# A four-layer cross-attention stack: 128x128 block products by Winograd's seven-product scheme in queries and outputs, and other buffers around layer 1's feed-forward part

## The chip, the cores and the metric

The kernel runs on one core of one Trainium2 chip. The core has five engines with a queue of instructions each: TensorE (PE), which multiplies matrices and loads its stationary operand by separate instructions (PEld), VectorE (DVE), ScalarE (ACT), GpSimd (POOL) and SyncE (SP), whose queue issues most of the DMAs. The metric is the device time of one execution in microseconds (us). All data are float32; one matmul of the program is two PE instructions.

## The reference

`x` is (4, 256, 256): four batch entries of 256 tokens of width 256. `ctx` is (4, 512, 128). Four layers each add a cross-attention and a feed-forward part (FFN), both on a layernormed `x`:

```
x = x + xattn_L(layernorm(x), ctx)
x = x + ffn_L(layernorm(x))            # L = 0, 1, 2, 3
```

Layer 0's attention has 16 heads of 16 and normed queries and keys, and its FFN picks 4 of 64 low-rank products per token. The attention of layers 1 to 3, which the change concerns, is

```
q = x @ Wq -> 16 heads of 128;   k, v = ctx @ Wk, ctx @ Wv -> 8 heads, each used by two
out = softmax(q @ k.T / sqrt(128)) @ v @ Wo
```

The FFN of layer 1 is a mixture of eight experts with two per token (hidden width 176) and a shared one; that of layer 2 has two experts, one of which is chosen per token; that of layer 3 runs for the 64 tokens of each batch entry that score highest in a router, and leaves the others.

## The kernel before

**Folded weights.** For layers 1 to 3 no keys and values are made. `folding` (L957) multiplies the weights of each head h once: `m_sb` holds Wq_h Wk_h^T / sqrt(128) (256x128) and `n_sb` holds Wv_h Wo_h (128x256). A head's scores are then ctx (M_h^T x), its output (p ctx) N_h. The weights for it come in four groups of four DMAs (`load_raw`, L941) into a pool of raw buffers.

**`attention` (L1674).** The work is cut into units (b, hp): one batch entry and one pair of heads, 32 per layer, 96 in all. `queries` multiplies M of two heads (as stationary 128x128 blocks) with the 256 tokens (`xnT`, transposed, 128x256 moving) into a PSUM bank `pq`, and ScalarE copies that to `qT` (128x512). It runs one unit ahead. `heads` makes the scores `ps` in four blocks of 128 context rows, their exponentials `pT` (ScalarE), the product `po` with the context, and its copy `oT`; POOL begins the sum of the exponentials (`half`, 128x1024). `summed` ends that sum on DVE (add, 32x32 transposes `turned`, reduction into `sums`). Four head pairs make a quarter here: `quotients` sums over partitions with PE (`pz`), takes reciprocals (`rz`), spreads them to `wide` with DVE and multiplies four `oT` by them, on POOL. It runs in head pair 5 for the first quarter of an entry, and in head pair 1 of the next entry for its second. `output` multiplies `oT` (stationary) with N (256 columns) over all 16 heads into a bank `py`, in head pair 3 of the next entry, one token tile of 128 after the other, and DVE adds it to `x_sb`. The layernorm of the next entry is spread over head pairs 2 (`Norm`, statistics), 4 (`tokens`) and 6 (`layernorm_T`: four PE transposes and a copy).

**The order of the work.** In these stages the orders of PE, ACT, DVE and POOL are those of the program text (`tc.manual_schedule`): what is written first stands first in the engine's queue. SP's order is the framework's. PSUM has eight banks: tags "s" (4), "mm" (2), "o" and "t" (1 each). A tile waits until the reads of the tile that had its buffer before are done; the buffers of a pool that is opened later may lie in the memory of a closed one, and then wait for what used that. A hook `after(b, hp)` puts pieces of the next FFN into units: layernorm and routing of entry b-1 in head pairs 4 to 7 of entry b (`beside1`, L1940; `beside2`, L2280; `beside3`, L2550, which has also pieces in head pairs 0 to 2). Of layer 3's router, `weights` ends with `diag` (L2436, DVE), which `spread` multiplies by ones (`pw`, L2443, PE).

**Layer 1's FFN** (from L1955). `Shared` units are the shared expert. `ranks`, `lists`, `listed` and `indices` make the list of rows for each expert (PE matmul `plist`, DVE). Then 23 blocks of 128 rows: each `Block` gathers its rows `xg` by an indirect DMA from `xd` in DRAM (POOL queue, four ahead), and writes its result to `yd` (SP queue). `Back` (L2162) gathers for each of eight token tiles its two rows from `yd` into `yg` (two indirect DMAs), and adds them to `x_sb`. It runs beside the fold of layer 2's weights, which PE does. Weights of the FFN come early into a pool `fwp` that is open from before attention 1. `load_raw(2, i)` (L2201) stands behind `indices` in the program.

Of the kernel before, what the change touches and what calls it, by code (L numbers as in the profile page):

```python
# [835 lines left out]
def bounded_path(ctx: ExitStack, tc: tile.TileContext, t, out: bass.AP, over):  # L836
# [815 lines left out]
    fwp = ctx.enter_context(tc.tile_pool(name="fwp", bufs=1))  # L1652
# [21 lines left out]
    def attention(L, m_sb, n_sb, first_xnT=None, after=None, at_end=None):  # L1674
# [4 lines left out]

        with tc.tile_pool(name=f"att{L}", bufs=2) as ap:  # L1680
            xnTs, xns, norms, qTs, outs, sums = {}, {}, {}, {}, {}, {}
            units = [(b, hp) for b in range(B) for hp in range(H // 2)]

            def queries(b, hp):
                u = f"{L}_{b}_{hp}"
                pq = bank("mm", [P, 2, S], f"pq{u}")
                for j in range(2):
                    for d in range(ND):
                        nc.tensor.matmul(  # L1689
                            pq[:, j, :],  # L1690
                            lhsT=m_sb[:, d, 2 * hp + j, :],
                            rhs=xnTs[b][:, d, :],
                            start=(d == 0),
                            stop=(d == ND - 1),
                        )
                qTs[b, hp] = ap.tile([P, 2 * S], F32, tag="qT", name=f"qT{u}")
                nc.scalar.copy(qTs[b, hp], pq.rearrange("p j s -> p (j s)"))  # L1697

            def heads(b, hp):
                u = f"{L}_{b}_{hp}"  # L1700
                pT = ap.tile([P, NK, 2 * S], F32, tag="pT", name=f"pT{u}")
                for k in range(NK):
                    ps = bank("s", [P, 2 * S], f"ps{u}_{k}")
                    nc.tensor.matmul(  # L1704
                        ps, lhsT=cT[:, b, k * P : (k + 1) * P], rhs=qTs[b, hp], start=True, stop=True
                    )
                    nc.scalar.activation(pT[:, k, :], ps, AF.Exp, bias=mbias[:, b, k : k + 1])  # L1707
                po = bank("o", [P, 2 * S], f"po{u}")
# [4 lines left out]
                raw = ap.tile([P, 2 * S], F32, tag="oT", name=f"oT{u}", bufs=H // 2 + 5)  # L1713
                nc.scalar.copy(raw, po)  # L1714
                outs.setdefault(b, []).append(raw)
# [15 lines left out]
            def quotients(b, quarter, last=False):  # L1731
# [10 lines left out]
                rz = ap.tile([P, 4, NB], F32, tag="rz", name=f"rz{u}")  # L1742
                nc.vector.tensor_scalar(rz, pz, 1.0e-37, None, ALU.max)  # L1743
                nc.vector.reciprocal(rz, rz)
                for i in range(4):
                    wide = ap.tile([P, NB, 32], F32, tag="turned", name=f"wide{u}_{i}")
                    nc.vector.transpose(wide, rz[:, i, :, None].to_broadcast([P, NB, 32]))  # L1747
# [935 lines left out]
```

## Time and profile before

Three runs took 1537.48, 1537.2 and 1531.69 us: median 1537.2. The profiled execution took 1532.39 us; its span, from the first to the last instruction of the trace, is 1530.6, and the rest lies around it. The mean granted clock of PE in it is 0.988 of full speed.

| engine | busy us | share of the span | instructions |
|---|---|---|---|
| PE | 1481.0 | 97% | 6243 |
| PEld | 935.2 | 61% | 6243 |
| DVE | 644.9 | 42% | 1357 |
| ACT | 589.1 | 38% | 1047 |
| POOL | 474.8 | 31% | 354 |

| stage | span, us | PE busy, us |
|---|---|---|
| attention 1 | 251 to 587 | 332.0 |
| FFN 1, shared expert and lists | 587 to 631 | 41.2 |
| FFN 1, blocks | 631 to 696 | 64.7 |
| FFN 1, rows back; fold; start of attention 2 | 696 to 740 | 38.4 |
| attention 2 | 740 to 1050 | 307.7 |
| FFN 2 and fold | 1050 to 1146 | 94.4 |
| attention 3 | 1146 to 1460 | 309.0 |
| end of attention 3 and FFN 3 | 1460 to 1530 | 59.1 |

In the profile's lines an instruction is named by its line in the kernel, its engine, and its tiles (out<-in, buffer numbers left out). In a group line there follow partitions x elements, the count, busy time in us and the mean in ns of one, then the idle time of the engine just before them and what ended it. In the timeline each line begins with start and duration in us; for several matmuls in a row the duration runs to the modelled end of the last, so the distance to the next start is the better measure. A line of waits has the total, the count and the longest. In a line of windows there follow, after the stretch, its length and the busy time and count of PE, PEld, DVE, ACT and POOL, PE's granted clock, the DMA share and GB/s.

### The profile page before, as it was taken

The page shows a single profiled execution, that of the slowest core. Times are in us where ns is not written, and L with a number is a line of the kernel's source. Part 1 is how long each engine was busy: PE and PEld are TensorE (multiplying, and loading weights), DVE is VectorE, ACT ScalarE, POOL GpSimd, SP SyncE. Part 2 cuts the span into 40 slices and gives each one's busy share as a digit, 9 for nine tenths or more (in the row PEclk, how much of TensorE's full clock was granted, in tenths as well). Part 3 has the DMA queues.
Part 4 walks back from the last instruction along what each step waited for, and adds up shares of the span by engine and source line. Part 5 has one row for each costly group of instructions (what it writes and reads, how often), then busy time and mean ns, then how long its engine had stood idle before and what let it go on. Part 6 is the DMA issues. An engine that isn't in the chain of part 4 may idle for free.

```text
span 1530.6 us, 16401 instructions
## 1 busy us (share of the span) xinstructions
PE 1481.0 (97%) x6243; PEld 935.2 (61%) x6243; DVE 644.9 (42%) x1357; ACT 589.1 (38%) x1047; POOL 474.8 (31%) x354
## 2 busy tenths in 40 slices
PE   8999998999999999999999999999999999999997
PEld 7665676556565567656455656566885565565656
DVE  5666863233534435424233332425442334324363
ACT  4666332442434433234444342422234433423221
POOL 2222343243434331324244342423002343423330
PEclk9999999999999999999999999999999999999999
DMA  4000223100000003135000000000410000000000
GB/s 159 1 1 2 69 69 126 16 0 0 7 1 7 0 3 115 56 86 163 7 0 1 0 1 0 1 0 3 140 55 1 0 1 0 0 1 1 0 0 31
DMA packets 39955, 43.15 MB, mean 28 GB/s; under 512 B 3833, under 2 KB 36826, under 8 KB 39868
## 3 DMA queue, kind: packets, MB, share of 16 engines
q1 hardware_dynamic: 36892, 35.85, 7.4%
q0 software_dynamic: 1872, 5.11, 1.2%
q8 instruction: 52, 0.85, 0.2%
q10 hardware_dynamic: 1104, 1.05, 0.2%
q14 instruction: 35, 0.29, 0.1%
HBM read 36.89 MB, written 5.11 MB: 27 GB/s over the span
## 4 chain that ended last, share of the span: by engine, by line
PE 84%; DVE 9%; POOL 3%; issue 2%; ACT 1%; DMA 0%; POOLq 0%; DVEq 0%; ACTq 0%
PE ps L1704 20%; PE po L1710 20%; PE pq L1689 10%; PE py L1760 10%; PE ph L2308 2%; PE po L2345 2%; PE pgu L2130 2%; PE ps L1313 2%; PE po L1323 2%; PE pyf L1440 1%; POOL oT L1751 1%; PE pyr L2155 1%; PE paf L1390 1%; DVE wide L1747 1%; POOL yg L2169 1%
## 5 line engine op out<-in xcount | busy, mean ns | idle before, releaser
L1717 POOL TENSOR_TENSOR half<-pT 128x1024 f32<-128x1024 f32 x96 | 225.0, 2344 | 579.1 <-ACT pT L1707 406.9
L1704 PE MATMUL ps<-qT,cT 128*128 128x512 f32 x768 | 350.1, 599 | 3.8 <-ACT qT L1697 3.8
L1710 PE MATMUL po<-pT,c_sb 128*128 128x512 f32 x768 | 345.3, 592 | 0.0
L1707 ACT ACTIVATE pT<-ps,mbias 128x512 f32<-128x512 f32 x384 | 263.3, 687 | 77.9 <-PE ps L1704 68.0
L1710 PEld LDWEIGHTS po<-pT,c_sb 128*128 128x128 f32 x768 | 146.0, 190 | 183.6 <-issue 183.1
L1704 PEld LDWEIGHTS ps<-qT,cT 128*128 128x128 f32 x768 | 147.7, 193 | 149.7 <-issue 140.6
L1723 DVE TENSOR_TENSOR half<-half 128x512 f32<-128x512 f32 x96 | 75.0, 782 | 357.4 <-POOL half L1717 357.4
L1689 PE MATMUL pq<-xnT_a,m_sb 128*128 128x256 f32 x768 | 183.4, 383 | 0.7 <-ACT xnT_a L923 0.7
L1760 PE MATMUL py<-n_sb,oT 128*128 128x256 f32 x768 | 169.3, 380 | 1.3 <-POOL oT L1751 1.3
L1689 PEld LDWEIGHTS pq<-xnT_a,m_sb 128*128 128x128 f32 x768 | 143.6, 191 | 39.8 <-issue 14.1
L1760 PEld LDWEIGHTS py<-n_sb,oT 128*128 128x128 f32 x768 | 145.4, 190 | 26.1 <-issue 4.8
L1714 ACT COPY oT<-po 128x512 f32<-128x512 f32 x96 | 56.2, 585 | 263.4 <-PE po L1710 263.4
L1697 ACT COPY qT<-pq 128x512 f32<-128x512 f32 x96 | 56.1, 585 | 255.5 <-PE pq L1689 246.5
L1751 POOL TENSOR_TENSOR oT<-oT,wide 128x512 f32<-128x512 f32 x90 | 121.0, 1375 | 67.3 <-DVE wide L1747 67.3
L1317 ACT ACTIVATE pT<-ps 128x512 f32<-128x512 f32 x128 | 66.1, 603 | 40.8 <-PE ps L1313 40.6
L1747 DVE STREAM_TRANSPOSE wide<-rz 128x512 f32<-128x512 f32 x96 | 65.1, 699 | 28.8 <-POOL oT L1751 28.0
L1725 DVE STREAM_TRANSPOSE turned<-half 128x512 f32<-128x512 f32 x96 | 68.3, 711 | 4.8
L1729 DVE TENSOR_REDUCE sums<-turned 128x16 f32<-128x512 f32 x96 | 65.8, 686 | 3.3
L1743 DVE TENSOR_SCALAR rz<-pz 128x64 f32<-128x64 f32 x24 | 5.4, 224 | 137.1 <-PE pz L1734 137.1
L1768 DVE TENSOR_TENSOR x_sb<-x_sb,py 128x256 f32<-128x256 f32 x24 | 10.1, 421 | 115.9 <-PE py L1760 115.9
L2110 POOL DMA_INDIRECT xg<-xd,who x23 | 22.0, 956 | 59.3 <-PE pxg L2118 33.0
L1313 PE MATMUL ps<-qT,kT 16*128 16x256 f32 x512 | 38.6, 408 | 0.0
(343 smaller groups left out, 1511.3 us busy)
## 6 DMA issues: line engine op xcount, KB each, us to landing
wo<-in_L_wo SPq DMA_DIRECT2D x13, 512.0 KB, 7.1
wq<-in_L_wqT SPq DMA_DIRECT2D x12, 512.0 KB, 4.1
yd<-yr SPq DMA_DIRECT2D x23, 128.0 KB, 1.7
w<-in_F_w SPq DMA_DIRECT2D x2, 1024.0 KB
wgu<-in_F_wgT SPq DMA_DIRECT2D x1, 1760.0 KB, 6.9
wgu<-in_F_wuT SPq DMA_DIRECT2D x1, 1760.0 KB, 10.8
wk<-in_L_wkT SPq DMA_DIRECT2D x12, 128.0 KB, 4.2
wv<-in_L_wvT SPq DMA_DIRECT2D x12, 128.0 KB, 5.9
```

The costliest lines, as they stand in the source:

```text
L1313: nc.tensor.matmul(ps[j][:, k, :], lhsT=kTs[b][r, hg, k0 : k0 + P], rhs=qTs[b][r, hg, :], start=True, stop=True)
L1317: nc.scalar.activation(pT[kp][:, j], ps[j], AF.Exp)
L1689: nc.tensor.matmul(pq[:, j, :], lhsT=m_sb[:, d, 2 * hp + j, :], rhs=xnTs[b][:, d, :], start=(d == 0), stop=(d == ND - 1),)
L1704: nc.tensor.matmul(ps, lhsT=cT[:, b, k * P : (k + 1) * P], rhs=qTs[b, hp], start=True, stop=True)
L1707: nc.scalar.activation(pT[:, k, :], ps, AF.Exp, bias=mbias[:, b, k : k + 1])
L1710: nc.tensor.matmul(po, lhsT=c_sb[:, b, k, :], rhs=pT[:, k], start=(k == 0), stop=(k == NK - 1))
L1717: nc.gpsimd.tensor_tensor(half, pT[:, 0:2], pT[:, 2:4], ALU.add)
L1723: nc.vector.tensor_tensor(part, half[:, 0], half[:, 1], ALU.add)
L1725: nc.vector.transpose(turned.rearrange("p f i -> p (f i)"), part)
L1747: nc.vector.transpose(wide, rz[:, i, :, None].to_broadcast([P, NB, 32]))
L1751: eng.tensor_tensor(oT, oT, wide.rearrange("p f i -> p (f i)"), ALU.mult)
L1760: nc.tensor.matmul(pys[c], lhsT=outs[b][h // 2][:, t0 : t0 + P], rhs=n_sb[:, h, :], start=(h == 0), stop=(h == H - 1),)
```

## The change

For the product of two matrices of 2x2 blocks (here of 128x128 each) eight block products are usual. The change takes Winograd's form of Strassen's scheme: seven products of sums of blocks, and sums of the products.

- **Queries.** `queries` makes seven products of 128x128x128 (`seven`) into two banks of tag "mm", `pa` (four products) and `pb` (three), and `four` puts the blocks of `qT` together: one ScalarE copy and four DVE adds. The sums of M's blocks (`m_sums`, DVE) are made two head pairs ahead during batch entry 0 of each layer, those of the tokens' blocks once per entry (`x_sums`, DVE). `first_queries` keeps the old form for head pairs 0 and 1 of entry 0. 90 of 96 units change.
- **Outputs.** They are made per quarter, three head pairs behind it: 7 products x 4 head pairs into two banks of tag "s", `four`, and one add to `x_sb`. The sums of `oT`'s blocks are four POOL operations of 128x128 per head pair (`o_sums`), those of N's blocks four per head pair on POOL during entry 0 (`n_sums`). The last quarter of a layer keeps the old form (`last_output`); 21 of 24 quarters change. `oT` has 9 buffers instead of 13.
- **Quotients.** `pz` stands between `ps` and `po` of head pair 4 or 0 of a unit; the `wide` transposes and the products on POOL are spread over that unit and the next. The steps of the layernorm move to head pairs 1, 3 and 5.
- **Layer 1's FFN.** The gathered rows `yg` get eight buffers instead of four; six `Back`s are issued at once and the last two after `Norm`. Gate and up weights lie in a pool of their own, `wd1` and `wd2` are loaded at the end of attention 1. The small tiles of the listing have their own pool, which is closed after `indices`; the raw buffers of layer 2's weights (`raw2`) are opened behind it, so that their loads wait for the listing's last reads. `fwp` is opened after FFN 1.
- **ScalarE's tables** are loaded by an explicit instruction: that of the exponential before the fold of layer 2 and in FFN 2, that of gelu in `end3`.

In PE instructions, a unit's queries go from 8 to 14 and a quarter's outputs from 32 to 56; the program has 7287 instead of 6243.

```diff
+            m_x = ap.tile([P, H // 2, 3, P], F32, tag="m_x", name=f"m_x{L}", bufs=1)
+            n_x = ap.tile([P, H // 2, 3, P], F32, tag="n_x", name=f"n_x{L}", bufs=1)
+            n_t3 = ap.tile([P, H // 4, P], F32, tag="n_t3", name=f"n_t3_{L}", bufs=1)
+            def s_sums(eng, a11, a12, a21, a22, s1, s2, s4):
+                eng.tensor_tensor(s1, a21, a22, ALU.add)
+                eng.tensor_tensor(s2, s1, a11, ALU.subtract)
+                eng.tensor_tensor(s4, a12, s2, ALU.subtract)
+                eng.tensor_tensor(a21, a11, a21, ALU.subtract)
+            def t_sums(eng, b11, b12, b21, b22, t1, t2, t4, t3=None):
+                eng.tensor_tensor(t1, b12, b11, ALU.subtract)
+                eng.tensor_tensor(t2, b22, t1, ALU.subtract)
+                eng.tensor_tensor(t4, b21, t2, ALU.subtract)
+                eng.tensor_tensor(b12 if t3 is None else t3, b22, b12, ALU.subtract)
+            def m_blocks(hp):
+                return [m_sb[:, d, 2 * hp + j, :] for j in range(2) for d in range(ND)]
+            def n_blocks(hp):
+                return [n_sb[:, 2 * hp + j, d * P : (d + 1) * P] for j in range(2) for d in range(ND)]
+            def x_blocks(b):
+                return [xnTs[b][:, d, c * P : (c + 1) * P] for d in range(ND) for c in range(NC)]
+            def o_blocks(oT):
+                return [oT[:, j * S + c * P : j * S + (c + 1) * P] for c in range(NC) for j in range(2)]
+            def m_sums(hp):
+                s_sums(nc.vector, *m_blocks(hp), *(m_x[:, hp, i, :] for i in range(3)))
+            def n_more(hp):
+                own = [n_t3[:, hp - H // 4, :]] if hp >= H // 4 else []
+                return [n_x[:, hp, i, :] for i in range(3)] + own
+            def n_sums(hp):
+                t_sums(nc.gpsimd, *n_blocks(hp), *n_more(hp))
+            def x_sums(b):
+                xxs[b] = ap.tile([P, 3, P], F32, tag="xx", name=f"xx{L}_{b}")
+                t_sums(nc.vector, *x_blocks(b), *(xxs[b][:, i, :] for i in range(3)))
+            def products(a, s, b, t):
+                (a11, a12, s3, a22), (s1, s2, s4) = a, s
+                (b11, t3, b21, b22), (t1, t2, t4) = b, t[:3]
+                if len(t) == 4:
+                    t3 = t[3]
+                return {
+                    1: (a11, b11), 2: (a12, b21), 3: (s4, b22), 4: (a22, t4), 5: (s1, t1), 6: (s2, t2), 7: (s3, t3)
+                }
+            def first_queries(hp):
...
+            def seven(of, u, tag="mm", between=None):
+                ps = []
+                for n, which in (("a", (1, 6, 7, 5)), ("b", (2, 3, 4))):
+                    if n == "b" and between:
+                        between()
+                    p = bank(tag, [P, len(which), P], f"p{n}{u}")
+                    for k, pair in enumerate(of):
+                        for at, i in enumerate(which):
+                            lhsT, rhs = pair[i]
+                            nc.tensor.matmul(
+                                p[:, at, :], lhsT=lhsT, rhs=rhs,
+                                start=(k == 0 and at == 0), stop=(k == len(of) - 1 and i == which[-1]),
+                            )
+                    ps.append(p)
+                return ps
+            def four(w, pa, pb):
+                nc.scalar.copy(w[:, 0, :], pa[:, 0, :])
+                nc.vector.tensor_tensor(w[:, 1, :], w[:, 0, :], pa[:, 1, :], ALU.add)
+                nc.vector.tensor_tensor(w[:, 2, :], w[:, 1, :], pa[:, 2, :], ALU.add)
+                nc.vector.tensor_tensor(w[:, 1::2, :], w[:, 1:3, :], pa[:, 3:4, :].to_broadcast([P, 2, P]), ALU.add)
+                nc.vector.tensor_tensor(w[:, 0:3, :], w[:, 0:3, :], pb, ALU.add)
+            def queries(b, hp):
+                of = products(
+                    m_blocks(hp), [m_x[:, hp, i, :] for i in range(3)],
+                    x_blocks(b), [xxs[b][:, i, :] for i in range(3)],
+                )
+                qTs[b, hp] = ap.tile([P, 4, P], F32, tag="qT", name=f"qT{L}_{b}_{hp}", bufs=3)
+                four(qTs[b, hp], *seven([of], f"q{L}_{b}_{hp}"))
+            def heads(b, hp, between=None):
...
+                if between:
+                    between()
...
+            oxs, rzs = {}, {}
...
+            def divided(b, hp, eng):
+                wide = ap.tile([P, NB, 32], F32, tag="turned", name=f"wide{L}_{b}_{hp}")
+                nc.vector.transpose(wide, rzs[b, hp // 4][:, hp % 4, :, None].to_broadcast([P, NB, 32]))
+                eng.tensor_tensor(outs[b, hp], outs[b, hp], wide.rearrange("p f i -> p (f i)"), ALU.mult)
+            def o_sums(b, hp, eng):
+                ox = oxs[b, hp] = ap.tile([P, 3, P], F32, tag="ox", name=f"ox{L}_{b}_{hp}", bufs=5)
+                s_sums(eng, *o_blocks(outs[b, hp]), *(ox[:, k, :] for k in range(3)))
+            class Output:
+                def __init__(self, b, quarter):
+                    self.b, self.u = b, f"{L}_{b}_{quarter}"
+                    self.of = [
+                        products(
+                            o_blocks(outs.pop((b, hp))), [oxs[b, hp][:, i, :] for i in range(3)],
+                            n_blocks(hp), n_more(hp),
+                        )
+                        for hp in range(4 * quarter, 4 * quarter + 4)
+                    ]
+                def products(self, between=None):
+                    self.ps = seven(self.of, f"o{self.u}", "s", between)
+                def add(self):
+                    w = ap.tile([P, 4, P], F32, tag="qT", name=f"w{self.u}", bufs=3)
+                    four(w, *self.ps)
+                    x = x_sb[self.b].rearrange("p c (e d) -> p (c e) d", d=P)
+                    nc.vector.tensor_tensor(x, x, w, ALU.add)
+            def last_output(b):
...
             xnTs[0] = first_xnT if first_xnT is not None else layernorm(0, f"a{L}_0")[1]
-            queries(*units[0])
+            first_queries(0)
             for n, (b, hp) in enumerate(units):
                 if b + 1 < B:
-                    if hp == 2:
+                    if hp == 1:
                         norms[b + 1] = Norm(b + 1, f"a{L}_{b + 1}")
-                    elif hp == 4:
+                    elif hp == 3:
                         xns[b + 1] = norms[b + 1].tokens()
-                    elif hp == 6:
+                    elif hp == 5:
                         xnTs[b + 1] = layernorm_T(xns[b + 1], f"a{L}_{b + 1}")
-                if n + 1 < len(units):
+                if n == 0:
+                    first_queries(1)
+                    x_sums(0)
+                elif n + 1 < len(units):
                     queries(*units[n + 1])
-                half = heads(b, hp)
-                if hp == 1 and b > 0:
-                    quotients(b - 1, 1)
-                if hp == 5:
-                    quotients(b, 0)
+                if b == 0:
+                    m_sums((hp + 2) % (H // 2))
+                last, i = ((b, 0), hp - 4) if hp >= 4 else ((b - 1, 1), hp)
+                prev = last[0] >= 0
+                h0 = 4 * last[1]
+                if prev and i == 1:
+                    for k in (2, 3):
+                        divided(last[0], h0 + k, nc.gpsimd)
+                    o_sums(last[0], h0, nc.gpsimd)
+                elif prev and i == 2:
+                    for k in (1, 2):
+                        o_sums(last[0], h0 + k, nc.gpsimd)
+                half = heads(b, hp, (lambda: quotients(*last)) if prev and i == 0 else None)
+                if prev and i == 0:
+                    for k in (0, 1):
+                        divided(last[0], h0 + k, nc.gpsimd)
+                if prev and i == 2:
+                    o_sums(last[0], h0 + 3, nc.gpsimd)
+                if b + 1 < B and hp == 6:
+                    x_sums(b + 1)
                 summed(b, hp, half)
-                if hp == 3 and b > 0:
-                    for c in range(NC):
-                        output(b - 1, c)
+                if b == 0:
+                    n_sums(hp)
+                if prev and i == 3:
+                    out = Output(*last)
+                    if last != (B - 1, 0):
+                        out.products()
+                        out.add()
                 if after:
                     after(b, hp)
-            output(B - 1, 0, 0, H // 2)
-            quotients(B - 1, 1, last=True)
+            out.products(lambda: quotients(B - 1, 1))
+            for k in range(4):
+                divided(B - 1, 4 + k, nc.vector if k % 2 else nc.gpsimd)
+            out.add()
             if at_end:
                 at_end()
-            output(B - 1, 1, 0, H // 2)
-            for c in range(NC):
-                output(B - 1, c, H // 2)
+            last_output(B - 1)
...
-            tc.tile_pool(name="back", bufs=4, side="right") as backp,
+            tc.tile_pool(name="back", bufs=N8, side="right") as backp,
             tc.tile_pool(name="f1", bufs=2) as fp,
-            tc.tile_pool(name="raw2", bufs=3) as rawp,
         ):
+            listing, later = ExitStack(), ExitStack()
+            lp = listing.enter_context(tc.tile_pool(name="f1l", bufs=1))
+            w1d = [fp.tile([P, NE, D], F32, tag=f"wd{i}", name=f"wd{i}", bufs=1) for i in (1, 2)]
+            wd1, wd2 = w1d
+            w1r = t["F1_wdT"][:FR, :].rearrange("(e f) n -> f e n", f=FE)
+            nc.sync.dma_start(wd1, w1r[:P])
+            nc.sync.dma_start(wd2[:FL], w1r[P:])
...
+            listing.close()
+            rawp = later.enter_context(tc.tile_pool(name="raw2", bufs=3))
             for i in range(4):
                 load_raw(2, i)
...
+            nc.scalar.preload_act_table_set("exp_and_others")
+            for n in range(N8 - 2):
+                backs[n] = Back(n)
             for n in range(N8):
-                backs[n] = Back(n)
...
                     xn = norm.tokens()
+                    for k in (N8 - 2, N8 - 1):
+                        backs[k] = Back(k)
...
+            later.close()
     f1s.close()
+    fwp = ctx.enter_context(tc.tile_pool(name="fwp", bufs=1))
...
+                if b + 2 == B:
+                    nc.scalar.preload_act_table_set("exp_and_others")
...
         def end3():
+            nc.scalar.preload_act_table_set("gelu_apprx_tanh_and_others")
```

## The prediction

> **What bounds the kernel now.** I read the page's first two parts, then the chain that ended last, the costliest groups, the timeline of one steady attention stretch, PE's waits, and the places where its granted clock falls.
>
> ```profile
> PE 1481.0 (97%) x6243; PEld 935.2 (61%) x6243; DVE 644.9 (42%) x1357; ACT 589.1 (38%) x1047; POOL 474.8 (31%) x354
> ...
> PE ps L1704 20%; PE po L1710 20%; PE pq L1689 10%; PE py L1760 10%; PE ph L2308 2%; PE po L2345 2%; PE pgu L2130 2%; PE ps L1313 2%; PE po L1323 2%; PE pyf L1440 1%; POOL oT L1751 1%; PE pyr L2155 1%; PE paf L1390 1%; DVE wide L1747 1%; POOL yg L2169 1%
> ```
>
> PE is busy 97% of the span, and the last chain runs mostly along it: queries (L1689) and outputs (L1760), which the change touches, are 10% of the span each. The timeline of PE in layer 2 (start, duration, both us) prices them:
>
> ```profile
> 775.03 1.89 PE L1689 MATMUL pq<-xnT_a,m_sb 128*128 128x256 f32 x8
> 776.75 3.60 PE L1704 MATMUL ps<-qT,cT 128*128 128x512 f32 x8
> 780.19 3.60 PE L1710 MATMUL po<-pT,c_sb 128*128 128x512 f32 x8
> 783.62 0.33 PE L1734 MATMUL pz<-sums,quad 128*128 128x64 f32 x2
> 784.27 0.66 PE L920 MATMUL pxn_a<-ident,xn_a 128*128 128x128 f32 x4 [0.32 <-DVE rz L1743]
> ...
> 836.55 13.98 PE L1760 MATMUL py<-n_sb,oT 128*128 128x256 f32 x64
> 850.36 1.89 PE L1689 MATMUL pq<-xnT_a,m_sb 128*128 128x256 f32 x8
> ```
>
> From start to start: queries 1.72 us, `ps` 3.44, `po` 3.43; a unit (one head pair of one batch entry) is 8.59. Outputs take 13.81 us for 64, 216 ns each; so do queries. The price of the new size, 128 columns with new weights each time, stands in the fold of layer 3's weights:
>
> ```profile
> 1141.15 1.05 PE L968 MATMUL pm<-wk,wq 128*128 128x128 f32 x8
> 1142.05 1.02 PE L989 MATMUL pn<-wo,wv 128*128 128x512 f32 x2
> 1142.90 1.15 PE L968 MATMUL pm<-wk,wq 128*128 128x128 f32 x8
> 1143.89 1.09 PE L989 MATMUL pn<-wo,wv 128*128 128x512 f32 x2
> ```
>
> 0.90/8 = 112 ns and 0.99/8 = 124 ns (in the second a weight load came late). Twice the columns cost 1.93 times as much.
>
> Where PE does stand still (its largest waits, then the start of attention 2, then the clock there):
>
> ```profile
> PE pw L2443 <- DVE diag L2436: 7.3, 4, 2.8
> PE ps L1704 <- ACT qT L1697: 3.8, 1, 3.8
> PE pxn_a L920 <- DVE rz L1743: 2.9, 9, 0.4
> PE py L1760 <- POOL oT L1751: 1.3, 2, 0.7
> ```
>
> ```profile
> 729.71 0.42 DVE L2177 TENSOR_TENSOR x_sb<-x_sb,yg 128x256 f32<-128x256 f32 x1 [0.54 <-DMA yg<-yd,where]
> 730.33 1.07 ACT L1697 COPY qT<-pq 128x512 f32<-128x512 f32 x2 [5.96 <-DVE x_sb L2177]
> 730.97 6.42 PE L1704 MATMUL ps<-qT,cT 128*128 128x512 f32 x8 [3.77 <-ACT qT L1697]
> ```
>
> ```profile
> 729.60:736.50 6.90, 5.54 (x7) 2.44 (x8) 0.42 (x1) 3.74 (x6) 0.00 (x0) 0.51 0.00 0
> ```
>
> The last line's 0.51 is the granted clock after that gap: these eight `ps` took 6.25 us (730.97 to 737.22), 2.8 more than the steady 3.44.
>
> **Queries.** 90 of 96 units change (hp 0 and 1 of batch entry 0 keep the old form in each layer): 8 matmuls at 216 ns = 1.73 us become 14 at 112 = 1.57: -0.16 x 90 = -14.4 us. At 109 ns (the closest pace of 128-column transposes) it is -18; at 124 ns, 1.736 against 1.728, +0.7.
>
> **Outputs.** 21 of 24 quarters (four head pairs) change: 32 matmuls, 6.91 us, become 56 at 112 ns, 6.27: -0.63 x 21 = -13.3 (-16.8 to +0.8 at the same bounds). Both go by the fold's row since it has that shape and new weights each time, and take 112 rather than 124 because late loads are rarer where operands wait in SBUF. PE thus loses 27.7 us of work (bounds -35 to +1.5).
>
> The Trainium skill ("TensorE: Matmul & The Clock Gate", section "Back-to-back issue gap") gives about 81 ns for a 128-column matmul in a stream of load-matmul pairs against 56 alone, and says that at this size the load has no room. By that ratio, 1.45, laid on half the 256-column price, an estimate, the products would run at 156 ns and cost +41 us in queries and +38 in outputs. The fold's rows, such pairs at 112 ns, speak against it here.
>
> **What the products need beside PE.** In the steady state all of this is costed at nothing; the cover is this. Per unit ScalarE's 128x512 copy (585 ns) becomes one of 128 columns (266, by `gsT`, L1989), and DVE gets four adds of 128, 128, 256, 384 columns in `four`: 0.285 (L2450) twice, 0.42 (L1768), 0.56 between that and L1723's 0.782 = 1.55 us. With `summed` (0.78+0.71+0.69) and a `wide` (0.70) DVE has 4.4 us per unit of 8.4; an output adds 1.55 + 0.78 per quarter, batch entry 0 four `m_sums` adds per unit (1.14). POOL has `half` 2.34 and a product with `wide` 1.38, and gets four `o_sums` of 128x128: none in the trace, so between 0.26 (a quarter of L985's 1.04 for 512 columns) and 0.73 (L1367, 256 columns); I take 0.37, half of the nearer row: 1.5 us, 5.2 of 8.4. Entry 0 adds four `n_sums` at the same price. Queues, not averages, decide: in the second unit of a quarter two products and an `o_sums` stand ahead of `half`, which then ends about 3 us late, and behind it `summed` and the next `four` on DVE. `queries` two units on needs the banks that `four` frees; steadily that leaves 2 x 8.4 - 11.8 = 5.1 us. So nothing waits, with some 2 us to spare; at 0.73 the spare is gone and entry 0 loses about 3 us per layer. For the router hooks (`tokens`, `weights`) that share these queues I charge +2 in all; bounds 0 and +12. The lower is no gain, since these queues hold up PE nowhere in the steady stretch.
>
> **Start of attention 2.** Before, the last `yg` gathers follow `Norm` on POOL, and the first `qT` copy waits until every gather has landed, since it reuses that memory. With eight buffers six `Back`s (twelve gathers, 1.25 us apart from 701.5) end at 716.5, where POOL stood idle until 716.8 anyway; four more follow to about 722.5, landing 2.8 us later, 725.3, before the first queries end at 727.2. Gap and half clock go: 3.8 + 2.8 = 6.6. What is late next is ScalarE's exp table (1.28 us), now loaded before the fold. I take -6; bounds -7 and +1 (gathers bunched at the first add).
>
> That clock agrees with the skill's rule ("TensorE: Matmul & The Clock Gate", section "What's actually happening"), half rate after about 3.4 us of idleness; by it, a gap cut below that window would refund the slow stretch too.
>
> **`pz`.** It moves between `ps` and `po`, and `layernorm_T` to another unit, so `rz` is off PE's path: -2.9 (9 waits); bounds -4.8 (0.53 each by start times) and 0.
>
> **Layer 3's hook.** `diag` waits on DVE behind four `wide`s that in turn wait for POOL (7.3 us in all, and two stretches at clock 0.51 of about 3.3 us, 1.7 lost in each). The `wide`s come earlier and in two portions, but `four` and `o_sums` join the same queues. Adding both up in queue order, `diag` is about 1 us nearer. I take -1; bounds -10 (all gone) and +7 (doubled).
>
> **Layer ends.** `pz` runs between the two halves of the products, hiding the first quotients: the 1.3 us of `py` goes. Bounds -1.3 and +3 (one 1.0-us wait per layer, as long as the longest of layernorm's).
>
> **FFN 1.** Twelve weight loads (3.84 MB), issued at 596 to 607 before, now wait for the listing to close at about 622 and stand on SP's queue ahead of the `yd` writes; they share the DMA engines with the first `xg` gathers (from 623.8, 2.8 us each). At the 326 GB/s they had, they take 11.8 us. PE needs the first rows at about 631. I take +1.5; bounds 0 and +8 (11.8 less the 4 us of room after a landing at 627). `wd1`, `wd2` and layer 2's FFN weights move too, with more than 15 us before their use: 0, or the +8 just named. The other preloads hide beside PE matmuls: 0, bounds -1.3 and +1.3, one table load.
>
> Sum: -27.7 + 2 - 6 - 2.9 - 1 - 1.3 + 1.5 = -35.4. The profiled execution took 1532.4 (span 1530.6), so 1497.0. The median of the runs shown is 4.8 above it, one run 0.7 below: the changed kernel could come out between 1496 and 1502. I say 1498; own range 1488 to 1508.
>
> **Rivals.** (a) *Late weight loads*: products at 124 ns. Then 1.5 instead of -27.7: 1526. For: one of the two rows above. Against: loads lie beside matmuls in the other row. Chance 0.06. (b) *The start of attention 2 stays*, because `qT` still reuses the gathers' memory: 1504. For: the wait is on the memory, not on the data. Against: gathers end earlier by POOL's idle time. Chance 0.15. (c) *DVE and POOL are late in the bunched units, hooks and entry 0*: +12 instead of +2, and the hook +7 instead of -1: 1516. For: `diag` already waits. Chance 0.13. (d) *Slower: POOL's and DVE's SBUF operations hold each other up.* `xn_f` (L908) took 970 ns where the same shape took 408, for `xn_a`. If `four` came later than the 5.1 us of slack, every unit would wait: place, the banks of `queries`; price, 1 us per us of lateness per unit, so 6.1 us late gives 90 - 35 = +55, 1587. It decides from 35.4 + 7.7 = 43 us over 90 units, 0.48 each: `half` 5.6 us late in every unit. Against: POOL would need 14.9 + 16p = 41.7 us per quarter, p = 1.67 us per add, over twice the 256-column row. Chance 0.09.
>
> **Numbers.** The likeliest has 0.57. Under 0.5% (7.7 us) a measurement of this kernel can't tell from none; (a) lies 11 us under the median, and half of it falls inside if the changed runs lie high. Faster 0.87, same 0.04, slower 0.09. The range reaches from 1484 (products nearer 109 ns, waits gone) to 1520 (over (c)); (d), (a) and some tails stay out.
>
> **What would show it.** Right: products 112 ns apart, units of 8.43 us, quarters' outputs of 6.3; no gap and full clock at attention 2; DVE near 870 us busy, POOL near 635. Wrong: PE waits before `pa` or `ps` on DVE's `four`, LDWEIGHTS of products in the gaps of PE, `xg` landing far above 2.8 us, `pw` waits of more than 3 us.

## The result: 1.25% slower, and the profile after

The changed kernel took 1555.35 us in the median of four runs (1554.1 to 1558.23), the kernel before 1537.34 beside it. The ratio is 1.0125, 95% interval 1.0094 to 1.0157; measured again, below, it was 1.0075. The prediction was 1498, with a range up to 1520 and 0.09 for slower. It was wrong.

PE does what was forecast of it. The head of the page, then its chain by lines:

```profile
span 1554.4 us, 19660 instructions
...
PE 1476.8 (95%) x7287; PEld 958.5 (62%) x7287; DVE 887.4 (57%) x1948; ACT 565.3 (36%) x1068; POOL 684.8 (44%) x786
...
PE 71%; DVE 17%; POOL 8%; issue 2%; ACT 1%; DMA 0%; another core or an unknown queue 0%; DVEq 0%; POOLq 0%; ACTq 0%
```

Before, the last chain ran over PE for 84% of the span, over DVE for 9 and POOL for 3. Now DVE and POOL have 25% between them: they have become the path somewhere. Not in the steady stretch. PE's timeline in layer 2 (start, duration):

```profile
768.00 0.38 PE L1771 MATMUL paq<-xnT_a,m_sb 128*128 128x128 f32 x2
768.22 0.39 PE L1771 MATMUL paq<-xx,m_x 128*128 128x128 f32 x2
...
769.56 3.60 PE L1801 MATMUL ps<-qT,cT 128*128 128x512 f32 x8
772.99 3.60 PE L1809 MATMUL po<-pT,c_sb 128*128 128x512 f32 x8
776.42 0.38 PE L1771 MATMUL paq<-xnT_a,m_sb 128*128 128x128 f32 x2
```

Fourteen products take 1.56 us (768.00 to 769.56), 111 ns each, and a unit 8.42 (768.00 to 776.42), where 8.43 was forecast and 8.59 measured before. PE's waits tell where the time is:

```profile
PE paq L1771 <- DVE xx L1703: 15.1, 9, 2.2
PE pw L2599 <- DVE diag L2592: 10.1, 4, 3.2
PE paq L1771 <- DVE xnT_a L1705: 7.9, 7, 2.3
PE pm L968 <- ACT m_sb L976: 6.6, 1, 6.6
```

Nine waits for `xx`: one in each layer at each change of batch entry, where the first products of the next entry need the sums of its tokens' blocks. The third line belongs to them: `xnT_a` L1705 is the fourth of these sums, written into a block of `xnT` itself. One of the nine, on all four engines (layer 1, entry 1 to 2):

```profile
395.09 0.69 ACT L1804 ACTIVATE pT<-ps,mbias 128x512 f32<-128x512 f32 x1 [0.17 <-PE ps L1801]
...
396.09 2.49 POOL L1850 TENSOR_TENSOR oT<-oT,wide 128x512 f32<-128x512 f32 x2 [1.55 <-DVE wide L1849]
...
400.42 2.35 POOL L1816 TENSOR_TENSOR half<-pT 128x1024 f32<-128x1024 f32 x1
...
402.81 0.93 DVE L1822 TENSOR_TENSOR half<-half 128x512 f32<-128x512 f32 x1 [6.21 <-POOL half L1816]
...
405.12 0.98 DVE L908 TENSOR_SCALAR xn_f<-x_sb,mv_f,rstd_f 128x256 f32<-128x256 f32 x2
...
407.18 0.55 DVE L1784 TENSOR_TENSOR qT<-qT,pbq 128x384 f32<-128x384 f32 x1
...
407.65 1.71 DVE L1702 TENSOR_TENSOR xx<-xnT_a 128x128 f32<-128x128 f32 x1
...
409.87 0.52 PE L1771 MATMUL paq<-xx,m_x 128*128 128x128 f32 x2 [2.19 <-DVE xx L1703]
```

The exponentials are done at 395.8 and POOL could begin `half`, but the two products with `wide` and four `o_sums` adds stand ahead of it, until 400.4: 4.6 us. DVE idles 6.2 us, then does `summed`, the FFN's layernorm, `four` and only then `xx`, whose first add takes 1.71 us instead of 0.29 because POOL's next `half` runs beside it. PE asks at 407.6 and goes on at 409.9. In layer 3, with `half` as late, the router's `diag` meets POOL's next `half` too, and one of its two operations takes 2.32 us instead of 0.28:

```profile
1311.35 2.33 POOL L1816 TENSOR_TENSOR half<-pT 128x1024 f32<-128x1024 f32 x1
1311.44 2.73 DVE L2592 TENSOR_SCALAR diag<-ident,wts 128x128 f32<-128x128 f32 x2
...
1313.82 0.90 PE L2599 MATMUL pw<-diag,ones 128*128 128x128 f32 x4 [2.79 <-DVE diag L2592]
```

Then the clock is gone as well. Windows around the first wait and around the one in layer 3 (after the stretch: its length, busy time and count of PE, PEld, DVE, ACT, POOL, then the granted clock):

```profile
407.40:413.40 6.00, 3.59 (x15) 3.02 (x15) 5.82 (x10) 0.89 (x3) 4.17 (x5) 0.73 0.07 23
1310.40:1320.90 10.50, 6.80 (x22) 4.56 (x21) 9.94 (x29) 0.85 (x2) 5.02 (x7) 0.71 0.00 0
```

To add such places up I take, for each matmul, the distance to the next one's start less the steady distance of its width (111 ns for 128 columns, 217 for 256, 431 for 512), and call it time over PE's own pace. It holds waits and lost clock alike. The profiled execution also stood still once for 7 us in the fold of layer 2 (the 6.6 us of `pm`), which no other profile shows; so this table uses the profile of the same kernel taken again (the first run below), against the kernel before:

| place | before | after | forecast difference |
|---|---|---|---|
| six changes of entry, layers 1 and 2 | 0 | 31.7 | 0 to +2 |
| layer 3, hook and changes of entry | 10.6 | 29.4 | -1 |
| fold and start of attention 2 | 9.2 | 3.1 | -6 |

With queries and outputs (-28.9, worked out below) and `pz` (-2.9) that makes 31.7 + 18.8 - 6.1 - 31.8 = +12.6, against the spans' 1542.2 - 1530.6 = +11.6.

### The profile page after: what moved, and what is told of

Same layout as the page of the kernel before. It is cut to its first block, busy times and chain, and to the rows that moved or that the text cites. A ratio compares the mean times of both kernels' runs of the same rounds, so it can differ in the third digit from the quotient of the medians.

```text
span 1554.4 us, 19660 instructions
## 1 busy us (share of the span) xinstructions
PE 1476.8 (95%) x7287; PEld 958.5 (62%) x7287; DVE 887.4 (57%) x1948; ACT 565.3 (36%) x1068; POOL 684.8 (44%) x786
## 4 chain that ended last, share of the span: by engine, by line
PE 71%; DVE 17%; POOL 8%; issue 2%; ACT 1%; DMA 0%; another core or an unknown queue 0%; DVEq 0%; POOLq 0%; ACTq 0%
PE ps L1801 17%; PE po L1809 13%; PE pao L1771 5%; PE paq L1771 4%; POOL half L1816 4%; PE pbo L1771 3%; PE pbq L1771 3%; DVE half L1822 2%; PE ph L2462 2%; PE po L2499 2%; POOL oT L1850 2%; PE pgu L2276 2%; PE ps L1313 2%; PE po L1323 2%; PE py L1886 1%
## 5 line engine op out<-in xcount | busy, mean ns | idle before, releaser
L1822 DVE TENSOR_TENSOR half<-half 128x512 f32<-128x512 f32 x96 | 100.5, 1047 | 280.8 <-POOL half L1816 280.8
L1771 PE MATMUL paq<-xx,m_x 128*128 128x128 f32 x360 | 73.0, 285 | 15.1 <-DVE xx L1703 15.1
L1771 PEld LDWEIGHTS paq<-xnT_a,m_sb 128*128 128x128 f32 x360 | 59.6, 196 | 38.4 <-PE po L1809 16.0
L1771 PE MATMUL paq<-xnT_a,m_sb 128*128 128x128 f32 x360 | 73.5, 287 | 9.8 <-DVE xnT_a L1705 7.9
L1780 ACT COPY qT<-paq 128x128 f32<-128x128 f32 x90 | 23.9, 265 | 121.4 <-PE paq L1771 119.5
L1771 PEld LDWEIGHTS paq<-xx,m_x 128*128 128x128 f32 x360 | 56.6, 198 | 17.0 <-DVE xx L1703 17.0
L1771 PE MATMUL pao<-n_x,ox 128*128 128x128 f32 x336 | 65.0, 275 | 0.0
L1784 DVE TENSOR_TENSOR qT<-qT,pbq 128x384 f32<-128x384 f32 x90 | 49.9, 554 | 9.4
L1697 POOL TENSOR_TENSOR ox<-ox,oT 128x128 f32<-128x128 f32 x84 | 49.3, 587 | 6.6
L1771 PE MATMUL pao<-n_sb,oT 128*128 128x128 f32 x264 | 51.2, 275 | 0.0
```

The source lines that it names most:

```text
L1771: nc.tensor.matmul(p[:, at, :], lhsT=lhsT, rhs=rhs, start=(k == 0 and at == 0), stop=(k == len(of) - 1 and i == which[-1]),)
L1822: nc.vector.tensor_tensor(part, half[:, 0], half[:, 1], ALU.add)
```

## The experiments

Theory A: the first products of an entry wait for `x_sums`, because DVE's queue is late behind POOL's `half`. Its rivals: DVE would be late anyway, so the wait would only move to `four`; POOL and DVE hold each other up at SBUF; or the part around layer 1's FFN is to blame. All ratios are to the kernel before on the same chip, with 95% intervals.

| kernel | median us | ratio |
|---|---|---|
| changed kernel, again | 1544.0 | 1.0075 (1.0050 to 1.0100) |
| `x_sums` one head pair earlier | 1510.9 | 0.9845 (0.9790 to 0.9899) |
| half first | 1485.9 | 0.9706 (0.9654 to 0.9758) |
| half first, again | 1489.7 | 0.9713 (0.9690 to 0.9736) |
| half first, products with `wide` ahead | 1507.6 | 0.9825 (0.9798 to 0.9852) |
| both edits | 1490.5 | 0.9724 (0.9702 to 0.9747) |
| both edits, queries in the old form | 1495.9 | 0.9753 (0.9727 to 0.9780) |
| half first, M's sums spread | 1488.1 | 0.9705 (0.9683 to 0.9726) |
| gathers as before | 1543.7 | 1.0067 (1.0042 to 1.0092) |
| FFN part alone | 1527.8 | 0.9964 (0.9938 to 0.9989) |

**The sums one head pair earlier.**

```diff
-                if b + 1 < B and hp == 6:
+                if b + 1 < B and hp == 5:
                     x_sums(b + 1)
```

> The changed kernel with the sums of the tokens' blocks (x_sums) made one head pair earlier, in head pair 5 instead of 6; nothing else moves. Theory A (the place: in head pair 6 these four adds stand on DVE behind a late summed and four, and the first products of the next entry wait for them, 2.2 to 2.5 us nine times, each followed by some 3 us at half clock): the six stretches of layers 1 and 2 (13.8 + 16.6 us over PE's own pace) and the first of layer 3 (7.0) go, the other two of layer 3 keep their wait of pw and lose about 1.5 each: -40, 1555 becomes 1515. Theory B (DVE as a whole is late behind POOL, so that the products would next wait for four): the gain is 10 or less, 1545 or more.

Ratio 0.9845, 1510.9, near theory A's number (1515). Against the changed kernel measured again (1.0075) that is 35 us less, where 40 were expected. The four adds now fall into DVE's idle time before `summed`; the waits for `xx` are gone, and `four`, which the rival had next in line, is waited for no more than in the changed kernel (2.5 and 1.9 us, L1784 and L1783, in both):

```profile
PE pw L2599 <- DVE diag L2592: 10.6, 4, 3.3
PE pn L989 <- DVE n_sb L992: 4.0, 2, 3.8
PE pxn_a L920 <- DVE xn_a L908: 2.5, 1, 2.5
PE ps L1801 <- DVE qT L1784: 2.5, 3, 0.9
PE paq L1771 <- DVE qT L1783: 1.9, 3, 0.7
```

`diag` stays: layer 3 still has its three stretches of 5.9 to 7.3 us.

**Half first.** Nothing but POOL's queue, and the `wide`s on DVE with it:

```diff
-                if prev and i == 1:
-                    for k in (2, 3):
-                        divided(last[0], h0 + k, nc.gpsimd)
-                    o_sums(last[0], h0, nc.gpsimd)
-                elif prev and i == 2:
-                    for k in (1, 2):
-                        o_sums(last[0], h0 + k, nc.gpsimd)
                 half = heads(b, hp, (lambda: quotients(*last)) if prev and i == 0 else None)
                 if prev and i == 0:
                     ...
+                elif prev and i == 1:
+                    for k in (2, 3):
+                        divided(last[0], h0 + k, nc.gpsimd)
+                    o_sums(last[0], h0, nc.gpsimd)
+                elif prev and i == 2:
+                    for k in (1, 2, 3):
+                        o_sums(last[0], h0 + k, nc.gpsimd)
-                if prev and i == 2:
-                    o_sums(last[0], h0 + 3, nc.gpsimd)
```

> The changed kernel with POOL's order turned round in the second and third unit of a quarter: half first, then the two products with wide and the o_sums. x_sums stays in head pair 6. Theory A' (half stands 4.3 us behind products and o_sums, and all of DVE's queue behind it: summed, the router's weights and diag, four, x_sums): the waits for xx in layers 1 and 2 go (-30) and those for diag in layer 3 as well, down to a rest of 2 us each (-22): 1555 becomes 1503. Rival (the wait of x_sums comes from DVE and POOL holding each other up at SBUF, half still runs beside x_sums): two thirds of the stretches stay, 1535 or more.

Ratio 0.9706, 0.9713 when measured again. `x_sums` and `diag` were left where they were; with `half` on time both waits nearly go. What is left of 15.1, 7.9 and 10.1 us:

```profile
PE paq L1771 <- DVE xx L1703: 2.5, 3, 0.8
...
PE pw L2596 <- DVE diag L2589: 1.3, 1, 1.3
PE paq L1771 <- DVE xnT_a L1705: 1.2, 5, 0.2
```

The three waits for `xx` stand in entry 0 of each layer, the one for `diag` in FFN 3 behind the attention. The same place as above (layer 1, entry 1 to 2):

```profile
387.09 2.35 POOL L1816 TENSOR_TENSOR half<-pT 128x1024 f32<-128x1024 f32 x1 [1.38 <-ACT pT L1804]
...
389.47 1.74 DVE L1822 TENSOR_TENSOR half<-half 128x512 f32<-128x512 f32 x1 [1.70 <-POOL half L1816]
...
395.45 2.44 POOL L1816 TENSOR_TENSOR half<-pT 128x1024 f32<-128x1024 f32 x1 [1.12 <-ACT pT L1804]
...
395.72 2.32 DVE L1704 TENSOR_TENSOR xx<-xnT_a,xx 128x128 f32<-128x128 f32 x1
...
398.36 0.39 PE L1771 MATMUL paq<-xnT_a,m_sb 128*128 128x128 f32 x2
...
398.58 0.39 PE L1771 MATMUL paq<-xx,m_x 128*128 128x128 f32 x2
```

`half` waits for ScalarE and not for POOL. `xx` is still held up by it, an add of 128x128 for 2.32 us, and PE does not notice. So the rival of SBUF is real. At `xx` it is not what changed: a sum of 1.7 to 2.3 us stands in seven of the nine places in the changed kernel, one of 2.3 to 2.4 in seven of them here. At `diag` it did change (2.32 to 0.29 us), so in layer 3 this run does not part the lateness from the hold-up that comes with it. DVE's add in `summed` (L1822) is even held up more: 1230 ns in the mean, 1047 in the changed kernel, 782 before. The page:

```profile
PE 1444.9 (97%) x7287; PEld 940.2 (63%) x7287; DVE 905.2 (61%) x1948; ACT 565.3 (38%) x1068; POOL 689.6 (46%) x786
...
PE 87%; DVE 9%; POOL 2%; issue 1%; ACT 1%; POOLq 0%; DVEq 0%; ACTq 0%
```

POOL and DVE are busier than in the changed kernel (689.6 against 684.8, 905.2 against 887.4), and the time is nearly 4% less: more work beside PE did not hinder it. I had expected 1503 and 2 us left at each `diag`; at the changes of entry there is none left.

**Half a dose.** Only the `o_sums` go behind `half`, the two products stay ahead:

```diff
+                if prev and i == 1:
+                    for k in (2, 3):
+                        divided(last[0], h0 + k, nc.gpsimd)
                 half = heads(b, hp, (lambda: quotients(*last)) if prev and i == 0 else None)
...
+                elif prev and i == 1:
+                    o_sums(last[0], h0, nc.gpsimd)
```

> A half dose of half first: the two products with wide stay ahead of half in the second unit of a quarter, only the o_sums go behind it, so half ends about 2.7 us late instead of 4.6. Theory A' (DVE's queue is late by what half is late): the waits for xx and diag fall from 2.2 to 2.9 us by 1.9 each to 0.3 to 1.0, and with them PE's clock stays full, since the waits of 0.8 to 1.0 us in the kernel with half first left it full: some 45 of the 70 us go, ratio 0.981. If the clock falls at any wait: 0.992.

0.9825; the 0.981 expected lies within its interval. The way there was not as expected. 36.5 us went (1544.0 to 1507.6) and not 45, and the clock did not stay full: in layer 3 all four places still lose some, 19.0 us over PE's own pace in sum, where the changed kernel lost 29.4. In layers 1 and 2 the waits for `xx` at entries 1 and 2 are gone; in entry 0 the first stays at 1.8 us and the second falls from 2.3 to 0.4. Its waits:

```profile
PE paq L1771 <- DVE xx L1703: 7.1, 5, 1.8
...
PE pw L2598 <- DVE diag L2591: 3.5, 4, 1.3
PE paq L1771 <- DVE xnT_a L1705: 3.2, 9, 0.5
```

`xx` is waited for 5 times instead of 9. Lateness of `half` of 4.6, 2.8 and 0.1 us in the second unit thus goes with ratios of 1.0075, 0.9825 and 0.971: a later `half`, a larger loss. It is no clean dose, since in the third unit `half` is 2.6 us late in the changed kernel and on time in both others.

**Both edits together.** Half first, and in it:

```diff
-                if b + 1 < B and hp == 6:
+                if b + 1 < B and hp == 5:
                     x_sums(b + 1)
```

> Half first and x_sums one head pair earlier, together. Theory A' leaves to the first edit only the waits for xx in entry 0 of each layer (0.8 to 1.0 us with their sequel 1.6, three times): -5, ratio 0.967 against 0.971 for half first alone. If the four adds, now on DVE just ahead of summed, delay it behind half or hold up POOL at SBUF: no gain, 0.971 or more.

0.9724: no better than half first alone, which lies inside the interval. Ahead of `summed`, the four adds push `diag` back by what they take, and layer 3 waits for it twice more (1.3 us each, once with lost clock: 3.8 and 2.2 us over PE's own pace). In entry 0 it saved little, 1.3 us over PE's own pace instead of 1.6 in each layer: PE now waits there for the sums of M's blocks.

**M's sums spread.** What was left in half first were three waits in entry 0, where four adds for M stand ahead of `x_sums`. The sums for head pairs 0 and 1 are made in head pairs 2 and 3:

```diff
-                if b == 0:
-                    m_sums((hp + 2) % (H // 2))
+                if b == 0 and hp < H // 2 - 2:
+                    m_sums(hp + 2)
+                if b == 0 and hp in (2, 3):
+                    m_sums(hp - 2)
```

> Half first, x_sums left in head pair 6, and the block sums of M for head pairs 0 and 1 made in head pairs 2 and 3 of entry 0 instead of 6 and 7, where they stood on DVE ahead of x_sums. Theory A': the last waits for xx (entry 0 of each layer, 1.6 us with their sequel) go, and nothing else changes: -4.8, ratio 0.968. If x_sums is held up by POOL's half instead of by m_sums, which it would now meet a little earlier: no change, 0.971.

Beside it the second run of half first: 

> Half first alone once more, beside the next kernel on one chip: ratio 0.971 again, within its interval of 0.965 to 0.976.

The waits for `xx` are gone from the profile, as expected; the gain of 4.8 us is below what the runs can tell (0.9705 against 0.9713). It is level with half first: 1488.1, with 1533.9 for the kernel before.

**Queries in the old form**, in the kernel with both edits; `first_queries` takes the batch entry as an argument:

```diff
                 if n == 0:
                     first_queries(1)
-                    x_sums(0)
                 elif n + 1 < len(units):
-                    queries(*units[n + 1])
-                if b == 0:
-                    m_sums((hp + 2) % (H // 2))
+                    first_queries(units[n + 1][1], units[n + 1][0])
...
-                if b + 1 < B and hp == 5:
-                    x_sums(b + 1)
```

> The kernel with both edits, but all queries in the old form (8 matmuls of 256 columns, one ScalarE copy; no m_sums, no x_sums, no adds on DVE for qT). Measures the first term of the sum by itself: 90 x (1.73 - 1.56) = 15 us of PE, so 15 us or 0.010 more than with both edits. If the products' sums and adds cost PE something that stays hidden in the profile, the difference is smaller; at 124 ns per product it would be 0.

0.9753 against 0.9724: the products in queries are worth some 4.5 us, not 15. The runs leave that uncertain by about 5 us; 15 lies outside. PE's own part is there: by distances between starts, queries take 157.0 us with products and 166.6 without, and 1260 products at 111.5 ns with 48 old matmuls would take 151.7, so 15 less 5.3, of which 4.1 are the waits in entry 0. The two waits of `diag` that `x_sums` brought take 6.0, 0.7 of it already in the 5.3: 15 - 5.3 - 5.3 = 4.4. Here the expectation failed, and for the reason of the whole case.

**The part around layer 1's FFN.** Alone, with attention as before. Of its edits to the kernel before, the core:

```diff
-            tc.tile_pool(name="back", bufs=4, side="right") as backp,
+            tc.tile_pool(name="back", bufs=N8, side="right") as backp,
...
+            listing, later = ExitStack(), ExitStack()
+            lp = listing.enter_context(tc.tile_pool(name="f1l", bufs=1))
+            w1d = [fp.tile([P, NE, D], F32, tag=f"wd{i}", name=f"wd{i}", bufs=1) for i in (1, 2)]
...
+            nc.scalar.preload_act_table_set("exp_and_others")
+            for n in range(N8 - 2):
+                backs[n] = Back(n)
             for n in range(N8):
-                backs[n] = Back(n)
```

> The kernel before with all of the change outside attention (buffers of layer 1's FFN, gathers, order of loads, table loads), queries and outputs as before. By the prediction's steps: -6 for the start of attention 2 and +1.5: 1533 against 1537. If the fold stands still for 7 us here too: 1540.

0.9964 (-5.7 us), as forecast. With the gathers of `Back` one by one and four buffers:

```diff
-            tc.tile_pool(name="back", bufs=N8, side="right") as backp,
+            tc.tile_pool(name="back", bufs=4, side="right") as backp,
...
-            for n in range(N8 - 2):
-                backs[n] = Back(n)
             for n in range(N8):
+                backs[n] = Back(n)
...
-                    for k in (N8 - 2, N8 - 1):
-                        backs[k] = Back(k)
```

> The changed kernel with the gathers of Back issued one token tile at a time in four buffers, as before. Tests the 7 us that PE stands still in the fold of layer 2 (717.5 to 726.7). If the twelve gathers in a row cause it: these 7 us go, the gap at the first qT copy with its half clock (6.6) comes back: 1555, no change. If the weight loads that fall into the same stretch cause it: the 7 us stay and 6.6 come on top: 1562. If it was an accident of one execution: 1555 + 6 - 0 and the stretch shows nothing of it.

1.0067, as the changed kernel again (1.0075). None of the three outcomes named came: the 7 us are absent, and so is the 6.6. The gap at the first `qT` copy did not come back:

```profile
730.98 0.59 ACT L1758 COPY qT<-pq 128x512 f32<-128x512 f32 x1 [1.19 <-issue]
731.05 1.16 POOL L2315 DMA_INDIRECT yg<-yd,where  x1 [0.30 <-DVE xx L1702]
...
732.46 2.74 PE L1801 MATMUL ps<-qT,cT 128*128 128x512 f32 x6
732.51 0.95 POOL L2315 DMA_INDIRECT yg<-yd,where  x1 [0.30 <-issue]
```

The copy runs while gathers are still being issued. Their order is not what removed the wait. The change's other pools may lay that buffer in other memory, which was not tried by itself. Attention's new form with the old FFN part was not tried.

**The changed kernel again.** 

> The changed kernel again, beside the others on one chip. The 7 us in which PE stands still in the fold of layer 2 (717.5 to 726.7) were seen in its profile and in none of the four variants since. If they were an accident of that execution: the fold shows under 4 us over PE's own pace and the ratio to before is about 1.010. If they belong to this kernel: they are there again.

1.0075, and the fold shows 3.1 us over PE's own pace. Of the profiles only the first has the 7 us:

```profile
719.14 1.02 PE L989 MATMUL pn<-wo,wv 128*128 128x512 f32 x2
...
726.73 2.08 PE L968 MATMUL pm<-wk,wq 128*128 128x128 f32 x8 [6.56 <-ACT m_sb L976]
```

What caused them stays open, and so does whether the other three runs of the first measurement had them too. All four took 1554.1 to 1558.2, the five of the second 1543.3 to 1548.4. Of the 12.2 us between the two profiles' spans 9.4 lie in the fold and the start of attention 2, and 4.3 ahead of attention 1.

## Why the prediction was wrong, step by step

- **Queries and outputs on PE: right.** 111 ns per product (112 forecast): 90 x (1.728 - 1.56) = 15.1. A quarter of outputs, 56 products, takes 6.25 us (406.79 to 413.04 in half first), 6.27 forecast: 21 x (6.905 - 6.25) = 13.8. Sum 28.9 against 27.7. Rival (a), late loads, did not come.
- **"So nothing waits, with some 2 us to spare": the step that failed.** The 5.1 us of room were worked out for `four`, which the unit after next needs, and `four` was indeed hardly waited for (4.4 us in all). The 11.8 us taken off in that sum are not worked out in the text. `x_sums` uses the same DVE queue one place further back and is needed by the next unit. The prediction counts neither its adds nor a wait for it. Its room, by the rows above: `xx` would have been done 4.6 + 1.4 us sooner, at 404.5, without the lateness and the hold-up, and PE asked at 407.6: 3.1 us. Lateness alone was 4.6. The hold-up, 1.4 of the 2.2 us of wait there, came on top; no run has the lateness without it. One size was off as well: `half` ends 4.6 us late and not 3. The work ahead of it is near what was priced (4.3 us from 396.1 to 400.4, against 2 x 1.38 + 1.5 = 4.2; an `o_sums` add takes 0.46 to 0.59 and not 0.37), but none of it is done before the exponentials are, since the products wait for `wide` on DVE.
- **The lost clock had no term.** I took the half clock after gaps as something the change removes, and did not charge it to waits that it brings. Of the 7.5 us at the entry change of layer 3 shown above, 2.8 are the wait for `diag`, 0.9 those for `four` and `xx`, and most of the rest is clock: products 0.43 to 0.58 us apart in pairs, instead of 0.22.
- **Layer 3's hook: -1 forecast, +18.8 measured.** `diag` was put about 1 us nearer, a sum whose terms the text does not give. `diag` stands behind `summed`, so it is late by what `half` is late, and it grew from 283 to 1124 ns in the mean, three times beside POOL's `half`.
- **Start of attention 2: -6 forecast, -6.1 measured,** but not for the reason given (eight buffers and the order of gathers), as the run with the old order shows. The line of the changed kernel's first profile that answers to the 3.77 us of before:

```profile
744.16 3.70 PE L1801 MATMUL ps<-qT,cT 128*128 128x512 f32 x8 [0.36 <-ACT qT L1758]
```

- **FFN 1, `pz`, layer ends: right in sum.** The FFN part alone gave -5.7 (forecast -4.5); `pxn_a` follows `po` without a wait; `py` waits 0.8 us instead of 1.3 (1.8 in half first).
- **The rivals.** (c) had the places, the bunched units, the hooks and entry 0, but priced them at +12 and +7, where 31.7 and 18.8 were measured. (d) named a slower end, by hold-ups at SBUF that make `four` late in every unit. The hold-ups came, but the waits were for `xx` and `diag`, at the changes of entry. Theory A in its first form, the place of `x_sums`, was only half the cause: moving it gave 0.9845, moving `half` alone 0.971.

The Trainium skill has the hold-up: "SBUF — State Buffer", section "Who interferes with whom", says that a DVE instruction with two SBUF inputs contends with a GpSimd instruction that reads SBUF, and that whoever issues first has the ports for the whole instruction. The `xx` rows (2.32 us beside a `half` of 2.44) agree. The rule speaks against putting sums on both engines, as this change does; in the run with half first the hold-up at these rows cost PE no wait.

## What to carry to other kernels

When work moves from the engine that bounds to engines with time to spare, check each new operand by its own deadline: what stands ahead of it in its queue, and which instruction needs it first; averages of busy time and the room of a neighbour in the same queue did not show it here. Put the long operation that others wait for ahead of short ones that nobody needs yet. A wait of 2.2 us on the bounding engine cost up to 4.7 here, where its clock fell.

## What the runs showed of the hardware

- **Clock.** At entries 1 and 2 of layers 1 and 2, in the changed kernel's first profile, gaps of 2.2 us and 0.2 shortly after came with half clock for 3.4 us at three of the four places (0.73 over 6 us above). At the fourth (493.9 to 497.5) it stayed at 1.00; in the second profile it fell there too. Gaps of 1.8 and 0.4 us in the half dose left it at 1.00 over 5 us in layers 1 and 2 and took it to 0.82 over 6.7 us in layer 3. Gaps of 1.1 and 0.6 us in the kernel with both edits took it to 0.79 over 7 us once. The length of a gap alone does not decide. "TensorE: Matmul & The Clock Gate" of the Trainium skill, section "HAM oscillation — how this bites in real kernels", gives gaps over about 3.4 us as the rule; these were shorter. In the kernel before, too, the clock at the start of attention 2 was half from 729.6 on, 2.4 us into the gap of 3.8, and not only after it.
- **The start.** The same kernel, half first, began attention 1 (`pxn_a`) at 252.5 us in one profile and at 259.3 in the other, 6.8 us apart, with the same code. The clock tells them apart: before that it was half for 10.2 us in all in the first and for 23.9 in the second, and half of the difference is 6.8. The stretch from 22 to 27 us (columns as in the windows above), here in the first profile:

```profile
22.00:27.00 5.00, 4.85 (x42) 4.00 (x40) 3.74 (x6) 3.38 (x7) 2.89 (x5) 1.00 0.42 133
```

And in the second:

```profile
22.00:27.00 5.00, 5.00 (x17) 4.34 (x17) 2.82 (x7) 1.36 (x2) 2.80 (x6) 0.53 0.25 79
```

The kernel before took between 1527 and 1540 us in its runs; that this has the same cause is likely and was not shown.
